# LN statistics of both possible token values taken in the first pass, and a nodes' loop in a written order with the W_res product behind it

## The chip, the cores and the metric

The kernel runs on one core of one Trainium2 chip. The metric is the device time of one execution in microseconds (us). The kernel before takes 3175.62 us, the median of three runs (3175.58 to 3176.56).

## The reference, cut to what matters

There are 6250 nodes (tokens) with 256 features each, and 100000 edges sorted by destination. Four blocks follow each other, each behind a LayerNorm without weights and each added to its input:

```python
x = x + L0_gnn(layernorm(x), edges)        # graph block
x = x + L0_ffn(layernorm(x))               # FFN of the tokens with the greatest router weight
x = x + L1_gnn(layernorm(x), edges)        # graph attention block
x = x + L1_ffn(layernorm(x))               # eight experts, weighted

# L0_ffn: weights = u @ wr + br;  the k - 1 tokens of the greatest weights are chosen
#   y = (gelu(u @ w1 + b1) @ w2 + b2) * weight;   result: u + y where chosen, u elsewhere
# L1_gnn: xn = layer_norm(x, ln1_g, ln1_b)
#   h = xn @ W;  a_src, a_dst: h with att_src, att_dst, for 8 heads
#   e = leaky_relu(a_src[src] + a_dst[dst]);  alpha = softmax of e over the edges of each dst
#   out = sum of h[src] * alpha + xn @ W_res + bias;  then a LayerNorm and an FFN with gelu
```

So a token entering L1_gnn is `X + weight * y` if it was chosen, and `X` if not. Which of the two it is can only be known once the weights of all tokens are there.

## The kernel before

The nodes lie in 50 tiles of 125 (NP = 125, NT = 50). Each tile has up to 17 slots of 128 edges (SL = 17). X, the running features, stays in SBUF for all tiles.

**First pass** (about 160 to 1226 us). `edges0(t)` gathers the source rows of a tile from DRAM, one indirect DMA per slot, issued by POOL (L342) into a ring of five buffers. VectorE builds a one-hot of the destinations (L401) and TensorE sums rows into nodes with it (L404). `weigh0(t0, c)` takes the router weight of each token of a chunk of tiles, normalises X and transposes it; `ffn0(t0, c)` makes the FFN value y of every token and stores it in the DRAM table `ytab` (L477 is y's addition). `weave` interleaves the three for successive chunks. The chunks' last two (tiles 47 to 49) have their `ffn0` beside the selection.

**Selection** (1226 to 1261). `select` finds the threshold weight by rounds of counting on VectorE and TensorE; `wm` (L583) is then the weight where the token was chosen and zero elsewhere.

**Nodes' loop** (1262 to 1385). All of `ytab` is loaded back into ten Y tiles, by SP and ACT queues in turn. `mix` makes X + wm*Y (L613), and its mean and variance (bn_stats L177, bn_aggr L178) and the inverse root by Newton steps (L166 to L172), for five tiles at a time. `front` normalises on ScalarE (L623), transposes on TensorE (L627) and applies ln1_g and ln1_b on ScalarE (L629). Two products follow for each tile, `ph` with W and the two attention columns (L651) and `pr` with W_res (L653). ScalarE evicts ph into `ht` (L654), VectorE copies the attention columns (ASAD, L655) and makes `rr` = pr + bias (L656). `ht` goes to the DRAM table `htab`, `rr` to `rtab`. Running maxima of ASAD go to `ext`. The scheduler orders the engines here, and puts into this loop also the fourteen X += cst of `add_o` (L915, on POOL) that belong to the second pass. After the loop a short chain over `ext` (L672 to L692) gives a shift for the softmax and a flag `f1I`, which is read into registers for a branch (L698).

**Second pass** (1393 us to the end). It has a written order on TensorE, VectorE and ScalarE. A tile has three groups of six slots (GS = 6; the last group ends with the nodes' own rows). `fetch(s)` gathers the rows of group s from `htab` with POOL (L342) into a ring of four buffers; `fetch_tile(t)` loads the tile's destination list (`ohT`) and `rr`. VectorE turns the list into a one-hot (L766), TensorE spreads the destination terms `adsh` over the edges (`pa`, L774), VectorE forms the logits (`ad`, L806), and the weighted rows are split in high and low parts (L859, L829) and summed on TensorE (L849). Behind it in the same weave run the block's FFN (L922, L933) and the eight experts (L1020, L1038).

Of the kernel before, what the change touches and what calls it, by code (L numbers as in the profile page):

```python
# [9 lines left out]
F32 = mybir.dt.float32  # L10
# [8 lines left out]
P = 128  # L19
N = 6250  # L20
E = 100000
D = 256
# [36 lines left out]
def gnn_ffn(ctx, tc, A, out):  # L59
# [100 lines left out]
    def rs(pool, dst, src, mul, add, op0=ALU.mult, name="rs"):  # L160

        p, n = src.shape[0], src.shape[-1]
        v = pool.tile([p, n], F32, name=name + "v")
        y = pool.tile([p, n], F32, name=name + "y")
        h = pool.tile([p, n], F32, name=name + "h")
# [19 lines left out]
    wm = stat.tile([NP, NT], F32, name="wm")  # L185
    sdT = edge.tile([P, 2, NT, SL], I32, name="sdT")
# [186 lines left out]
    with ExitStack() as p1:  # L373
# [63 lines left out]
        def weigh0(t0, c):  # L437
# [3 lines left out]
            for j in range(c):  # L441
# [11 lines left out]
                nc.vector.scalar_tensor_tensor(jk, z, 1.0, f_wr, op0=ALU.mult, op1=ALU.mult, accum_out=wts[:, t:t + 1])  # L453
                pt = psum.tile([P, KD, NP], F32, name="mi")
# [3 lines left out]
                yield  # L458

        def ffn0(t0, c):  # L460
# [11 lines left out]
            for j in range(c):  # L472
                y = pool.tile([NP, 1, D], F32, name="y")
                py = psum.tile([NP, D], F32, name="py", bufs=1)
                for f in range(NF):
                    nc.tensor.matmul(py, hT[f][:, j * NP:(j + 1) * NP], f_w2[:, f, :], start=(f == 0), stop=(f == NF - 1))  # L476
                nc.vector.tensor_tensor(y[:, 0, :], py, f_b2[0:NP, :], ALU.add)  # L477
                ndma(y, ytab, t0 + j, False)
                yield


        far = wp.tile([1, NT, HEADS], BF16, name="far")
        nc.sync.dma_start(wcat[:, :, 0:D], A["L1_gnn_W"].rearrange("(k p) m -> p k m", p=P))
        nc.sync.dma_start(wcat[:, :, HA:HA + D], A["L1_gnn_W_res"].rearrange("(k p) m -> p k m", p=P))
        atts = [bcast_load(wp, A["L1_gnn_" + n].rearrange("h j -> (h j)"), D, n) for n in ("att_src", "att_dst")]
# [3 lines left out]
        b2g = bcast_load(wp, A["L1_gnn_ffn_b2"], D, "b2g")  # L489
# [3 lines left out]
        for n, k in (("ln1_g", KD), ("ln1_b", KD), ("ffn_b1", NF), ("ln2_g", KD), ("ln2_b", KD)):  # L493
            r = wp.tile([k, P], F32, name=n + "r")
# [4 lines left out]
        bo_f = wp.tile([NEXP, D], F32, name="bo_f")  # L499
        bo_p = wp.tile([NEXP, 3, D], BF16, name="bo_p")  # L500
# [4 lines left out]
        row = {n: wp.tile([L2 + NEXP, D], F32, name="bn" + n) for n in ("g", "v", "b", "m", "be")}  # L505
# [6 lines left out]
        def prepare():  # L512
# [4 lines left out]
            yield from store_dloc(wp, psum, "mi")  # L517
            for a, att in enumerate(atts):
                for k in range(KD):
                    wa = wp.tile([P, D], F32, name="wa")  # L520
# [21 lines left out]
            rs(wp, v, v, 1.0, 1e-3, name="bq")  # L542
# [35 lines left out]
        nc.vector.tensor_scalar(wts, wts, f_br[0:NP, :], None, op0=ALU.add)  # L578


        sl = p1.enter_context(tc.tile_pool(name="sl", bufs=1))
        mask = select(tc, sl, psum, wts, ident, iota, ones, upto)
        nc.vector.tensor_tensor(wm, wts, mask, ALU.mult)  # L583
        for t0, c in CHUNKS0[-2:]:
            for _ in ffn0(t0, c):
                pass


    w2 = ctx.enter_context(tc.tile_pool(name="w2", bufs=1))
    with ExitStack() as md:  # L590
# [6 lines left out]
        for t0 in range(0, NT, XC):  # L597
            Y.append(wp.tile([NP, XC, D], F32, name=f"Y{t0}"))
            ndma(Y[-1], ytab, t0, True, eng=(nc.sync, nc.scalar)[(t0 // XC) % 2])
# [5 lines left out]
        MC = 5  # L605
        spans = [(0, 1), (1, 2), (3, 2)] + [(t, MC) for t in range(5, NT, MC)]

        def mix(t0, c):

            mv = pool.tile([NP, MC, 2], F32, name="mv")  # L610
            for j in range(c):
                t = t0 + j
                nc.vector.scalar_tensor_tensor(X[:, t, :], Y[t // XC][:, t % XC, :], wm[:, t:t + 1], X[:, t, :], op0=ALU.mult, op1=ALU.add)  # L613
                bn(pool, mv[:, j, :], X[:, t, :])
            r2 = pool.tile([NP, 2, MC], F32, name="r2", bufs=3)
            rs(pool, r2[:, 0, 0:c], mv[:, 0:c, 1], 1.0 + 1e-5, 1e-10)
            nc.vector.scalar_tensor_tensor(r2[:, 1, 0:c], mv[:, 0:c, 0], -1.0, r2[:, 0, 0:c], op0=ALU.mult, op1=ALU.mult)
            return r2

        def front(t, r2, j):  # L620

            z = pool.tile([NP, D], F32, name="z")
            nc.scalar.activation(z, X[:, t, :], AF.Identity, bias=r2[:, 1, j:j + 1], scale=r2[:, 0, j:j + 1])  # L623
            pt = psum.tile([P, KD, NP], F32, name="mi", bufs=3)
            xT = pool.tile([P, KD, NP], F32, name="xT", bufs=3)
            for k in range(KD):
                nc.tensor.transpose(pt[:, k, :], z[:, k * P:(k + 1) * P], ident[0:NP, 0:NP])  # L627
            for k in range(KD):
                nc.scalar.activation(xT[:, k, :], pt[:, k, :], AF.Identity, bias=ln1_b[:, k:k + 1], scale=ln1_g[:, k:k + 1])  # L629
            return xT  # L630

        stats = [mix(*spans[0])]
        fronts = []
        for s, (t0, c) in enumerate(spans):
            if s + 1 < len(spans):
                stats.append(mix(*spans[s + 1]))
            if s == 0:
                fronts.append(front(0, stats[0], 0))
            ht = pool.tile([NP, MC, HW], F32, name="ht")
            rr = pool.tile([NP, MC, D], F32, name="rr")  # L640
            for j in range(c):
                t = t0 + j
                if j + 1 < c:
                    fronts.append(front(t + 1, stats[s], j + 1))
                elif t + 1 < NT:
                    fronts.append(front(t + 1, stats[s + 1], 0))
                xT = fronts[t]
                ph = psum.tile([NP, HA], F32, name="ph")
                pr = psum.tile([NP, D], F32, name="pr")
                for k in range(KD):  # L650
                    nc.tensor.matmul(ph, xT[:, k, :], wcat[:, k, 0:HA], start=(k == 0), stop=(k == KD - 1))  # L651
                for k in range(KD):
                    nc.tensor.matmul(pr, xT[:, k, :], wcat[:, k, HA:HA + D], start=(k == 0), stop=(k == KD - 1))  # L653
                nc.scalar.activation(ht[:, j, :], ph[:, 0:HW], AF.Copy)  # L654
                nc.vector.tensor_copy(ASAD[:, t, :], ph[:, D:HA])  # L655
                nc.vector.tensor_tensor(rr[:, j, :], pr, g_bias[0:NP, :], ALU.add)  # L656
            ndma(ht[:, 0:c, :], htab, t0, False)
            ndma(rr[:, 0:c, :], rtab, t0, False)
            e1 = pool.tile([NP, MC, 2 * HEADS], F32, name="e1")
            nc.vector.tensor_copy(e1[:, 0:c, 0:HEADS], ASAD[:, t0:t0 + c, 0:HEADS])  # L660
            nc.vector.tensor_scalar(e1[:, 0:c, HEADS:], ASAD[:, t0:t0 + c, 0:HEADS], -1.0, None, op0=ALU.mult)
            e2 = ext if s == 0 else pool.tile([NP, 2 * HEADS], F32, name="e2")
            nc.vector.tensor_reduce(e2, e1[:, 0:c, :].rearrange("p t h -> p h t"), AX.X, ALU.max)
            if s:
                nc.vector.tensor_tensor(ext, ext, e2, ALU.max)
# [30 lines left out]

        mid.close()
# [9 lines left out]


        rem = keep.tile([NP, NT, 2 * HEADS], F32, name="rem")
# [864 lines left out]
```

## Time and profile before

| quantity | value |
|---|---|
| median of three runs | 3175.62 us |
| profiled execution | 3178.92 us |
| its span | 3177.1 us |
| mean granted TensorE clock | 0.947 |
| busy: TensorE, VectorE, ScalarE, POOL | 2804.1, 2016.2, 1198.4, 1934.0 us |

The profile is of one execution. Busy time is the time in which an engine has an instruction at work; an engine can be busy for most of the span and still bind only some of the stages. Line numbers are those of the kernel before. A wait is named by the engine and tile that waited and by the one that released it last.

### The profile page before, as it was taken

How to read it: one execution, taken by the hardware profiler on the slowest of the kernel's cores; microseconds unless marked ns; L12 is line 12 of the kernel's file. 1: busy time of each engine (PE TensorE's matmuls, PEld its weight loads, DVE VectorE, ACT ScalarE, POOL GpSimd, SP SyncE). 2: the span in 40 equal slices, each digit the busy share in tenths (PEclk: the TensorE clock that was granted, in tenths of full speed). 3: DMA queues.
4: the chain of work that ended last, by engine and by line, in shares of the span. 5: the costliest groups of instructions: out<-in, count | busy, mean ns of one | idle time of the engine just before them, and what ended most of it. 6: DMA issues, size and time to landing. Idle time of an engine off the chain costs nothing.

```text
span 3177.1 us, 40496 instructions
## 1 busy us (share of the span) xinstructions
PE 2804.1 (88%) x12746; PEld 1972.1 (62%) x12746; DVE 2016.2 (63%) x5670; ACT 1198.4 (38%) x2215; POOL 1934.0 (61%) x1772
## 2 busy tenths in 40 slices
PE   6278888888888896856889999999999999999999
PEld 5246566566666675746766666666666666666665
DVE  8543444444444346947888787777778777777731
ACT  5112222212212221634555455454544545445332
POOL 0277777777777771247777666666666666666400
PEclk8689999999999898977999999999999999999999
DMA  5533333333333335356655545445454454544412
GB/s 110 165 110 110 110 112 111 112 111 111 112 112 111 112 112 124 110 152 177 181 154 155 163 125 158 141 135 163 125 163 138 135 162 125 163 138 141 125 53 60
DMA packets 263977, 412.04 MB, mean 130 GB/s; under 512 B 55449, under 2 KB 202373, under 8 KB 263710
## 3 DMA queue, kind: packets, MB, share of 16 engines
q0 software_dynamic: 81600, 226.41, 25.7%
q1 hardware_dynamic: 169062, 170.03, 18.2%
q10 hardware_dynamic: 13080, 12.80, 1.7%
q8 instruction: 106, 1.74, 0.2%
q14 instruction: 129, 1.06, 0.1%
HBM read 376.61 MB, written 33.24 MB: 129 GB/s over the span
## 4 chain that ended last, share of the span: by engine, by line
PE 46%; DVE 6%; ACT 2%; issue 1%; DMA 1%; POOL 1%; DVEq 0%; ACTq 0%; SPq 0%; POOLq 0%
PE ph L1020 19%; PE py L1038 9%; PE iotaP L849 5%; PE py L933 5%; PE ph L922 5%; DVE hrow L839 1%; PE mi L895 1%; PE mi L960 1%; DVE lo L829 1%; POOL hrow L342 1%; PE pa L774 1%; DVE bnst L177 0%; DVE oh L861 0%; ACT hi L859 0%; DMA hrow<-htab,sdT 0%
## 5 line engine op out<-in xcount | busy, mean ns | idle before, releaser
L342 POOL DMA_INDIRECT hrow<-htab,sdT x850 | 1023.4, 1204 | 496.1 <-issue 214.2
L342 POOL DMA_INDIRECT rows<-gtab,sdT x850 | 808.1, 951 | 258.7 <-issue 125.8
L404 PE MATMUL ps<-rows,oh 128*125 128x257 f32 x1700 | 474.6, 416 | 84.8 <-DMA rows<-gtab,sdT 72.7
L1021 ACT ACTIVATE h<-ph,bi,sc 128x500 f32<-128x500 f32 (+3 forms) x448 | 321.6, 723 | 539.0 <-PE ph L1020 538.8
L404 PEld LDWEIGHTS ps<-rows,oh 128*125 128x125 f32 x1700 | 321.1, 201 | 229.6 <-DMA rows<-gtab,sdT 143.3
L1020 PE MATMUL ph<-h,W 128*128 128x500 f32 (+3 forms) x896 | 372.6, 549 | 0.0
L1038 PE MATMUL py<-Wo,h 128*125 128x256 f32 x1600 | 370.2, 381 | 0.4 <-ACT h L1021 0.4
L1020 PE MATMUL ph<-wcat,W 128*128 128x500 f32 (+3 forms) x896 | 363.5, 544 | 2.4 <-ACT h L1021 2.3
L1038 PEld LDWEIGHTS py<-Wo,h 128*125 128x125 f32 x1600 | 297.0, 188 | 72.3 <-issue 28.1
L839 DVE TENSOR_TENSOR hrow<-hrow 128x768 f32<-128x768 f32 x300 | 280.2, 975 | 76.4 <-ACT hrow L824 76.4
L1041 DVE SCALAR_TENSOR_TENSOR X<-py,gate,X 125x256 f32<-125x256 f32 x400 | 173.4, 477 | 203.4 <-PE py L1038 203.2
L829 DVE TENSOR_TENSOR lo<-hrow,hi 128x792 fp32r<-128x792 f32 (+1 forms) x300 | 285.3, 992 | 0.2 <-issue 0.2
L859 ACT ACTIVATE hi<-hrow 128x792 fp32r<-128x792 f32 (+1 forms) x300 | 236.7, 823 | 123.7 <-DVE hrow L839 123.2
L849 PE MATMUL iotaP<-hi,oh 128*125 128x264 f32 x850 | 252.0, 329 | 0.0
L1020 PEld LDWEIGHTS ph<-wcat,W 128*128 128x128 f32 x896 | 160.6, 192 | 140.2 <-issue 109.8
L1020 PEld LDWEIGHTS ph<-h,W 128*128 128x128 f32 x896 | 160.2, 195 | 106.3 <-issue 95.8
L849 PE MATMUL iotaP<-lo,oh 128*125 128x264 f32 x850 | 219.7, 291 | 4.9 <-DVE lo L829 4.8
L467 PE MATMUL ph<-xT,f_w 128*128 128x500 f32 (+3 forms) x448 | 191.4, 553 | 0.5 <-ACT xT L457 0.5
L922 PE MATMUL ph<-xT,h_w 128*128 128x500 f32 (+3 forms) x448 | 186.3, 558 | 4.3 <-ACT hT L924 3.3
L476 PE MATMUL py<-f_w,hT 128*125 128x256 f32 x800 | 182.8, 381 | 1.2 <-DVE y L477 0.4
L933 PE MATMUL py<-h_w,hT 128*125 128x256 f32 x800 | 177.6, 380 | 0.0
L849 PEld LDWEIGHTS iotaP<-lo,oh 128*125 128x125 f32 x850 | 162.5, 191 | 20.6 <-issue 7.9
(305 smaller groups left out, 3742.5 us busy)
## 6 DMA issues: line engine op xcount, KB each, us to landing
W<-in_L_ffn_W SPq DMA_DIRECT2D x224, 256.0 KB
Wo<-in_L_ffn_Wo SPq DMA_DIRECT2D x112, 256.0 KB
ohT<-dltab SPq DMA_DIRECT2D x50, 535.5 KB
rows<-gtab,sdT POOLq DMA_INDIRECT x850
hrow<-htab,sdT POOLq DMA_INDIRECT x850
hrow<-htab SPq DMA_DIRECT2D x50, 115.5 KB
X<-in_x ACTq DMA_DIRECT2D x10, 560.0 KB
ytab<-y SPq DMA_DIRECT2D x50, 112.0 KB
```

What stands on the lines that cost most here:

```text
L342: nc.gpsimd.indirect_dma_start(out=dst, out_offset=None, in_=tab, in_offset=bass.IndirectOffsetOnAxis(ap=idx, axis=0))
L404: nc.tensor.matmul(ps, oh[:, i, :], rows[:, i, :], start=(s0 + i == 0), stop=(s0 + i == SL - 1))
L467: nc.tensor.matmul(ph[:, 0:n], f_w1[:, k, f * P:(f + 1) * P], xT[:, k, 0:n], start=(k == 0), stop=(k == KD - 1))
L829: nc.vector.tensor_tensor(L["lo"][:, c], L["rows"][:, c], L["hi"][:, c].bitcast(F32), ALU.subtract)
L839: nc.vector.tensor_tensor(h4, h4, rows[:, c, D:, None].to_broadcast([P, GS // 2, HEADS, HD]), ALU.mult)
L849: nc.tensor.matmul(tiles[t]["ps"], L["oh"][:, i, :], r[:, i, :], start=(g + i + q == 0), stop=(g * GS + i == SL - 1 and q == 1))
L859: nc.scalar.activation(L["hi"][:, c], L["rows"][:, c], AF.Copy)
L922: nc.tensor.matmul(ph[:, 0:n], h_w1[:, k, f * P:(f + 1) * P], C["xT"][:, k, 0:n], start=(k == 0), stop=(k == KD - 1))
L933: nc.tensor.matmul(py[:, i, :], C["hT"][f][:, j * NP:(j + 1) * NP], h_w2[:, f, :], start=(f == 0), stop=(f == NF - 1))
L1020: nc.tensor.matmul(ph[:, 0:n], w[:, k, f * P:(f + 1) * P], rhs[:, k, 0:n], start=(k == 0), stop=(k == KD - 1))
L1021: nc.scalar.activation(h[:, f, 0:n], ph[:, 0:n], AF.Relu, bias=cols[1][:, f, e:e + 1], scale=cols[0][:, f, e:e + 1])
L1038: nc.tensor.matmul(py[:, i, :], hidden[u, "2"][:, k, j * NP:(j + 1) * NP], weights[u, "Wo"][:, k, :], start=(k == 0), stop=(k == KD - 1))
```

## The change

Three things are done.

1. In the first pass, `weigh0` keeps the mean and the variance of each normalised token in `mv2`, and `ffn0` forms x2 = X + weight*y and takes its mean and variance too. `roots_of` turns the variances into inverse roots for both cases. After the selection a blend by the mask leaves the right pair of scale and shift for each token in `r2`, so the nodes' loop takes no statistics. The router's bias is added chunk by chunk.
2. The nodes' loop has a written order on TensorE, VectorE, ScalarE and POOL. One in three normalisations and one half of each gain run on VectorE. ASAD is copied from `ht` for five tiles at a time, and the maxima are taken at tiles 20, 40, 48 and 50. The W_res product is taken out: it follows, for two tiles at a time, after the maxima's chain and before the branch, from the transposed tiles, which are kept in the Y buffers (`xTs`). The attention terms `adsh` are made inside that stage (`terms`).
3. The pool `w3` with the ring of the second pass is opened ahead of the nodes' loop. The gathers of its first four groups are issued right behind the loop, and the first tile's one-hot is made there. In the second pass two of three fetches stand half a step earlier.

The core of the diff:

```diff
@@ weigh0
+                nc.vector.tensor_copy(mv2[:, 0, t, 0:1], mv[:, 0:1])
+                nc.vector.scalar_tensor_tensor(mv2[:, 0, t, 1:2], mv[:, 1:2], r1[:, 2:3], r1[:, 2:3], op0=ALU.mult, op1=ALU.mult)
...
+            nc.vector.tensor_scalar(wts[:, t0:t0 + c], wts[:, t0:t0 + c], f_br[0:NP, :], None, op0=ALU.add)
@@ ffn0
                 ndma(y, ytab, t0 + j, False)
+                t = t0 + j
+                x2 = pool.tile([NP, D], F32, name="x2", bufs=1)
+                nc.vector.scalar_tensor_tensor(x2, y[:, 0, :], wts[:, t:t + 1], X[:, t, :], op0=ALU.mult, op1=ALU.add)
+                bn(pool, mv2[:, 1, t, :], x2)
                 yield
+        def roots_of(a, b, name):
+            rs(wp, r2[:, :, 0, a:b], mv2[:, :, a:b, 1], 1.0 + 1e-5, 1e-10, name=name)
+            nc.vector.scalar_tensor_tensor(r2[:, :, 1, a:b], mv2[:, :, a:b, 0], -1.0, r2[:, :, 0, a:b], op0=ALU.mult, op1=ALU.mult)
@@ around the selection
-        nc.vector.tensor_scalar(wts, wts, f_br[0:NP, :], None, op0=ALU.add)
+        roots_of(0, CHUNKS0[-2][0], "ra")
+        ready.close()
         sl = p1.enter_context(tc.tile_pool(name="sl", bufs=1))
         mask = select(tc, sl, psum, wts, ident, iota, ones, upto)
...
+        roots_of(CHUNKS0[-2][0], NT, "rb")
+        nc.vector.tensor_tensor(wm, wts, mask, ALU.mult)
+        nc.vector.tensor_tensor(part, r2[:, 1], mask[:, None, :].to_broadcast(both2), ALU.mult)
+        nc.vector.tensor_scalar(mask, mask, -1.0, 1.0, op0=ALU.mult, op1=ALU.add)
+        nc.vector.tensor_tensor(r2[:, 0], r2[:, 0], mask[:, None, :].to_broadcast(both2), ALU.mult)
+        nc.vector.tensor_tensor(r2[:, 0], r2[:, 0], part, ALU.add)
@@ nodes' loop
+        mid.enter_context(tc.manual_schedule(engines={PE, DVE, Activation, Pool}))
-                nc.vector.scalar_tensor_tensor(X[:, t, :], Y[t // XC][:, t % XC, :], wm[:, t:t + 1], X[:, t, :], op0=ALU.mult, op1=ALU.add)
-                bn(pool, mv[:, j, :], X[:, t, :])
-            rs(pool, r2[:, 0, 0:c], mv[:, 0:c, 1], 1.0 + 1e-5, 1e-10)
...
+        def norm(t):
+            r, m = (r2[:, 0, q, t:t + 1] for q in range(2))
+            zs[t] = pool.tile([NP, D], F32, name="z", bufs=4)
+            if t % 3 == 2:
+                nc.vector.tensor_scalar(zs[t], X[:, t, :], r, m, op0=ALU.mult, op1=ALU.add)
+            else:
+                nc.scalar.activation(zs[t], X[:, t, :], AF.Identity, bias=m, scale=r)
...
+        def gain(t):
+            pt = pts.pop(t)
+            nc.scalar.activation(xTs[t][:, 0, :], pt[:, 0, :], AF.Identity, bias=ln1_b[:, 0:1], scale=ln1_g[:, 0:1])
+            nc.vector.tensor_scalar(xTs[t][:, 1, :], pt[:, 1, :], ln1_g[:, 1:2], ln1_b[:, 1:2], op0=ALU.mult, op1=ALU.add)
...
+        steps = ((8, <X + wm*Y of the tile>),
+                 (0, product), (3, turn), (-1, evict), (2, gain), (5, norm))
+        for i in range(-8, NT + 1):
+            for lead, f in steps:
+                if 0 <= i + lead < NT:
+                    f(i + lead)
+        for k in range(len(ring)):
+            fetch_edges(k)
+        nc.vector.tensor_scalar(ext[:, HEADS:], ext[:, HEADS:], -1.0, None, op0=ALU.mult)
+        first_onehot()
@@ behind the maxima's chain, ahead of the branch
+        for t in range(0, NT, 2):
+            pr = psum.tile([NP, 2, D], F32, name="pr")
+            for i in range(2):
+                for k in range(KD):
+                    nc.tensor.matmul(pr[:, i, :], xTs[t + i][:, k, :], wcat[:, k, HA:HA + D], start=(k == 0), stop=(k == KD - 1))
...
+            nc.vector.tensor_tensor(rr[:, j:j + 2, :], pr, g_bias[0:NP, None, :].to_broadcast([NP, 2, D]), ALU.add)
+            if j == 2 or t + 2 == NT:
+                ndma(rr[:, 0:j + 2, :], rtab, t - j, False)
+            if t == 10:
+                terms()
@@ second pass
-            if s >= 1:
+            if s >= 2 and (s - 1) % NG == 0:
                 fetch(s + len(ring) - 2)
...
+            if s >= 1 and s % NG != 0:
+                fetch(s + len(ring) - 1)
```

## The prediction

> **What bounds the kernel now.** I read the page's busy shares first, then a table of stretches, because shares are averages over stages with different limits. A row of the table has the stretch, its length, the busy time of each engine in it, the granted TensorE clock, the DMA share and GB/s.
>
> ```profile
> PE 2804.1 (88%) x12746; PEld 1972.1 (62%) x12746; DVE 2016.2 (63%) x5670; ACT 1198.4 (38%) x2215; POOL 1934.0 (61%) x1772
> ```
>
> ```profile
> core 0: us, PE busy (x) PEld busy (x) DVE busy (x) ACT busy (x) POOL busy (x), PEclk, DMA share, GB/s
> 160.00:1200.00 1040.00, 896.33 (x3473) 633.63 (x3472) 446.78 (x1948) 215.57 (x432) 788.37 (x829) 0.94 0.39 111
> 1226.00:1262.00 36.00, 16.52 (x88) 14.33 (x88) 27.82 (x84) 3.02 (x9) 1.09 (x4) 0.72 0.69 166
> 1262.00:1270.00 8.00, 0.00 (x0) 0.00 (x0) 8.00 (x42) 0.00 (x0) 0.00 (x0) 0.50 1.09 247
> ...
> 1300.00:1340.00 40.00, 34.06 (x163) 26.91 (x161) 39.83 (x188) 25.79 (x65) 9.44 (x5) 1.00 0.37 109
> 1340.00:1384.00 44.00, 43.31 (x215) 36.27 (x216) 18.94 (x73) 32.41 (x83) 11.78 (x5) 1.00 0.40 119
> 1388.00:1413.00 25.00, 0.00 (x0) 0.00 (x0) 6.76 (x17) 0.00 (x0) 13.47 (x14) 0.51 0.65 170
> ...
> 1443.00:1600.00 157.00, 126.85 (x746) 110.61 (x746) 120.60 (x281) 81.50 (x152) 116.33 (x100) 0.87 0.65 182
> ...
> 1800.00:3040.00 1240.00, 1232.60 (x5555) 819.90 (x5554) 962.91 (x2088) 595.25 (x928) 782.93 (x628) 1.00 0.50 142
> ```
>
> From 1800 us TensorE is full: nothing there can be moved by this change. The nodes' loop is VectorE-bound to 1340 and TensorE-bound after. From 1388 to 1413 TensorE does nothing: the second pass waits for its first gathers and first one-hot. The first pass (160 to 1200) looks loose on every engine, but its timeline on POOL says otherwise:
>
> ```profile
> 601.67 0.95 POOL L342 DMA_INDIRECT rows<-gtab,sdT  x1 [0.30 <-issue]
> 602.93 1.10 POOL L342 DMA_INDIRECT rows<-gtab,sdT  x1 [0.30 <-PE ps L404]
> 604.34 0.95 POOL L342 DMA_INDIRECT rows<-gtab,sdT  x1 [0.30 <-PE ps L404]
> ```
>
> A gather every 1.25 us (0.95 and 0.30 to issue) without a longer pause: 829 gathers fill 1040 us. POOL's issue paces the first pass; TensorE and VectorE have slack.
>
> **First pass.** Each tile gains on VectorE a copy and a small product (0.15 and 0.16 us, like L414 and L170), x2 (0.48, like L432), and bn_stats with bn_aggr (0.42 and 0.18): 1.4 us, 70 us over the pass. VectorE is busy 43% of it, so the cover is the gathers' pace; if VectorE were the pace it would cost all 70. What can leak through is a gather that gets longer. The row: of 830 gathers, 14 took over 1.0 us, 2.2 us too much in all, and ten of these fell on the X product of L432 and its bn_stats, which come 50 times (the 1.10 above is one; L432 ran at 602.73). So 50 new pairs x 10/50 x 0.16 = 1.6 us. The rule against it: the Trainium skill (SBUF — State Buffer, "Who interferes with whom") says that a VectorE instruction with two SBUF inputs contends with a GpSimd instruction that reads SBUF, and that the later one blocks for the whole of the other. By it each x2 could hold the gathers for its 0.48: 24 us. I take the row, 1.6, and keep 24 for the range.
>
> **Tail and select.** The gathers end at 1204; then VectorE's chain counts. In the compiled order the roots of tiles 0 to 46 (12 operations of 125x94, 0.22 each, by the 125x50 rows of 0.19 to 0.24) stand ahead of the last tile's one-hot: +2.7. Inside the threshold search come x2 and bn of three tiles (3.2) and the last roots (2.5); about 2.1 of these fill the 0.7 us in which VectorE waits for TensorE's counts in each round: +3.6. After the search come four operations of 0.2 to 0.27: +1.1. With the gathers' 1.6 the search ends 9 us later: 1261.4 becomes 1270.4. Bounds 3 (all in waits) and 13 (nothing in waits).
>
> **Y loads: a new wait.** Before, SP and ACT issue them from 1240 and they land under the search. In the changed order all ten stand behind the last operation after the search, since their buffers are now those that it uses: 6.25 MB start at 1270.4. Queued behind them on SP are only the htab stores, 15 us away; ACT's engine waits too, but has nothing else then; h_w1, h_w2 and the first one-hot's load are ahead and land under the search. The first two blocks (1.25 MB at the 247 GB/s of the 1262:1270 row: 5.1 us, and 1.7 to land, like the hrow load at 1393.54) are there at 1277.2. Then X 0.48, z 0.59, transposes 0.4, the two half gains 0.45 and 0.28 (VectorE's waits for ACT's in the compiled order) and handoffs, 1 us: first product at 1280.4. Later blocks come at 0.5 us a tile, which is faster than the loop.
>
> **Loop.** These rows give its pitch:
>
> ```profile
> L629 ACT ACTIVATE xT<-mi,ln_bc,ln_gc 128x125 f32<-128x125 f32 x100 | 40.1, 452 | 25.1 <-PE mi L627 25.0
> L623 ACT ACTIVATE z<-X,r 125x256 f32<-125x256 f32 x50 | 29.6, 593 | 35.5 <-DVE r L617 35.3 <-DVE rsh L171 0.2
> L915 POOL TENSOR_TENSOR X<-X,cst 125x1024 f32<-125x1024 f32 x11 | 26.1, 2368 | 70.5 <-ACT z L623 43.9 <-DVE rsh L171 15.3 <-DVE X L613 7.2
> L613 DVE SCALAR_TENSOR_TENSOR X<-Y,wm,X 125x256 f32<-125x256 f32 x50 | 24.9, 500 | 0.4 <-DVE wm L583 0.4
> L654 ACT ACTIVATE ht<-ph 125x264 f32<-125x264 f32 x50 | 19.2, 385 | 7.8 <-PE ph L651 7.5
> ```
>
> TensorE: the tile's pitch in 1340:1384 is 2.0 us; the W_res product is 0.87 of it (32 matmuls of the same 256 columns, L933, take 6.99), so 1.13 stays. ACT: 0.39 + 0.45 + 2/3 of 0.59 = 1.23. VectorE: X 0.48, a third of a 0.40 normalisation, gain 0.28 (between L655's 0.165 for 16 columns and L656's 0.41 for 256), copies and maxima 0.08: 0.97. But POOL's 14 X+=cst still run in the loop, and they stop VectorE:
>
> ```profile
> 1327.28 2.37 POOL L915 TENSOR_TENSOR X<-X,cst 125x1024 f32<-125x1024 f32 x1 [7.95 <-DVE rsh L171]
> ```
>
> ```profile
> 1327.57 2.10 DVE L172 SCALAR_TENSOR_TENSOR rsy<-rsh,rsy 125x5 f32<-125x5 f32 x1
> ```
>
> A 0.15 us operation took 2.10, to POOL's end. Summed over the loop's small operations by their normal 0.15, such excess is 15 us of POOL's 29.9. The same rule of the skill would give all 29.9: (48.5 + 29.9)/50 = 1.57 us a tile; the row gives (48.5 + 15)/50 = 1.27. I take 1.35, nearer the row, a little up because the X products are now a larger part of what VectorE meets POOL with. 50 x 1.35 = 67.5: last eviction at 1348.5, against 1383.6.
>
> **W_res product.** It moves behind the loop. The maxima's chain comes first (1385.4 to 1388.2 before): 1351.8. Its 25 additions (some 0.7 each, twice L656's columns) and 13 pairs of rtab stores on SP run beside it; nothing waits behind these stores but the second pass's own loads. 50 x 0.87 = 43.7 us on TensorE alone, with 3.5 lost while VectorE makes terms() (7 us, of which two free PSUM buffers cover 3.5): 1399. The last addition and the branch, 4 us (before: 1388.1 to 1392.8, with its flag read at the end; now the flag is old): 1403. So product and loop together take what they took; the branch comes some 10 us later than before.
>
> **What is won** lies behind the branch. POOL's gathers of the first four groups (23 x 1.25 = 29 us) start when htab is stored, at 1351, and end at 1380 under the product; the first one-hot and terms() are done too. Before, the first VectorE step of the second pass (ad, L806) ran at 1413.8:
>
> ```profile
> PEld L774 <- DVE ohT L766: 26.6, 1, 26.6
> ...
> DVE ohT L766 <- DMA rr<-rtab: 13.6, 1, 13.6
> ```
>
> TensorE waited 26.6 us for the first one-hot, and that 13.6 for the loads issued with it. Now ad runs at 1403: -10.8. The gathers' lead (before, rows of group 2 came at 1428.5) and the earlier fetches in the ramp (1443:1600, TensorE 81%) I put at 2. On SP the second pass's loads follow the branch as before. Weights: first used at 1467, issued at 1399; 10 us later and 11 earlier leaves 45. Sum: -13, made against the profiled execution (3178.9, span 3177.1 and 1.8 around it), which stands 3.3 above the median; the difference goes onto the median: 3175.6 - 13 = 3162.6.
>
> **Rivals.**
> 1. The loop's gain is eaten by blocking: 1.57 us a tile (+11) and the late bound of the select (+4) give about 3177. For it: the 2.10 above; against it: only half of POOL's time hit VectorE before, when VectorE was at 99.6%.
> 2. The gathers are held by x2 (the slower side). Place: the first pass, POOL's pace. Price: 0.48 x 50 = 24 instead of 1.6, +22: 3185. It decides from 0.26 us a tile (13/50). For it: POOL has no slack at all there. Against it: the 602.93 row, a stretch of 0.15 only, in one pair of five.
> 3. More is won: loop at 1.2 us (-7.5) and the ramp, where POOL is busy 116 of 157 us plus 30 of issue, takes up more of the gathers' lead (-8): 3147.
> 4. The change doesn't do what it says: the gathers stay behind the branch. Not so in the compiled order; they stand ahead, and the flag's read waits for none of them.
>
> **How the numbers follow.** Forecast 0.50 (own range -5 to -21: 3155 to 3171), rival 1 0.20, rival 2 0.15, rival 3 0.15. About 0.2%, 6.4 us, is what a measurement can tell from no change. Faster: 0.45 of the forecast and rival 3, 0.60. Same: 0.05 of the forecast and 0.11 of rival 1. Slower: the rest of rival 1 and rival 2, 0.24. Range 3143 to 3186: rival 3 with some room below, rival 2 above.
>
> **What would show it.** Right: gathers of the first pass still 1.25 us apart; first X of the loop near 1277; last eviction near 1348; 23 gathers ahead of the branch; ad near 1403. Wrong: rows gathers above 1.0 us in the mean (rival 2); POOL's X+=cst with a VectorE operation of 2 us beside each (rival 1); TensorE waiting in the W_res product; an ad at 1403 but a second tile end no earlier than before, which would mean that the ramp, not the start, sets the pace.

## The result, and the profile after

The changed kernel takes 3190.98 us (median of 5 runs, 3189.86 to 3193.59), the kernel before 3175.58: a ratio of 1.0051, 95% interval 1.0036 to 1.0066. It is slower, where 3162.6 was forecast; the range ended at 3186. The profiled execution has a span of 3191.8 us, 14.7 more than before.

The busy shares of the page and the table of stretches (columns as in the prediction) stand against those of before:

```profile
PE 2805.2 (88%) x12746; PEld 1975.2 (62%) x12746; DVE 2068.1 (65%) x5677; ACT 1169.0 (37%) x2149; POOL 1926.3 (60%) x1772
```

```profile
core 0: us, PE busy (x) PEld busy (x) DVE busy (x) ACT busy (x) POOL busy (x), PEclk, DMA share, GB/s
160.00:1200.00 1040.00, 889.60 (x3442) 632.83 (x3443) 501.35 (x2170) 213.70 (x429) 787.88 (x830) 0.93 0.39 112
...
1262.00:1270.00 8.00, 1.20 (x4) 0.99 (x4) 6.87 (x26) 0.00 (x0) 1.09 (x4) 0.50 0.48 159
1270.00:1300.00 30.00, 2.70 (x10) 2.33 (x10) 10.70 (x36) 0.00 (x0) 0.00 (x0) 0.50 0.80 194
1300.00:1340.00 40.00, 37.77 (x182) 28.77 (x183) 37.09 (x77) 32.69 (x84) 18.56 (x10) 0.93 0.50 133
...
1388.00:1413.00 25.00, 21.28 (x85) 18.07 (x86) 11.07 (x16) 0.00 (x0) 11.12 (x11) 0.86 0.61 168
...
1443.00:1600.00 157.00, 121.03 (x727) 105.86 (x728) 125.49 (x288) 76.79 (x145) 111.48 (x96) 0.85 0.62 174
1800.00:3040.00 1240.00, 1232.72 (x5564) 819.61 (x5563) 962.50 (x2074) 597.58 (x934) 793.87 (x638) 1.00 0.50 143
```

VectorE did 55 us more in the first pass and POOL kept its pace there; the hole in TensorE at 1388 to 1413 is filled. But a new one has come: from 1262 to 1300 TensorE works 4 us of 38. The second pass from 1800 on is what it was. So the loss lies in places, and these moments (us from the start of the span) say in which:

| | before | predicted | after |
|---|---|---|---|
| first gather of the first pass | 134.9 | 134.9 | 144.2 |
| last gather of the first pass | 1202.9 | 1204.5 | 1210.3 |
| threshold search begins | 1226.2 | | 1243.2 |
| search and what follows it end | 1261.4 | 1270.4 | 1280.7 |
| first X product of the loop | 1262.0 | 1277.2 | 1287.8 |
| first eviction for htab | 1274.8 | (first product 1280.4) | 1304.2 |
| last eviction for htab | 1383.6 | 1348.5 | 1368.7 |
| last W_res product ends | 1384.5 | 1399 | 1424.3 |
| ad, first step of the second pass | 1413.8 | 1403 | 1430.6 |
| from ad to the end of the span | 1763.3 | 1761 | 1761.2 |

A moment is where an instruction starts, but for the rows that say "end". The last row is the point: nearly all that was gained or lost lies ahead of ad, and ad came 16.8 later instead of 10.8 earlier. Four places carry it.

**The start.** ACT's timeline, before and after (start, duration, engine or its queue, line, operation):

```profile
21.57 12.24 ACTq L82 DMA_DIRECT2D X<-in_x  x9
33.84 1.28 ACT L292 ACT_TABLE_LOAD   x1 [33.84 <-DMA X<-in_x]
```

```profile
21.34 20.11 ACTq L82 DMA_DIRECT2D X<-in_x  x9
41.49 1.28 ACT L291 ACT_TABLE_LOAD   x1 [41.49 <-DMA bnm<-in_L_ffn_m]
```

and SP's timeline after:

```profile
24.82 0.38 SPq L140 DMA_DIRECT2D att_src<-in_L_gnn_att_src  x1
...
39.38 0.29 SPq L522 DMA_DIRECT2D bnbe<-in_L_ffn_be  x1
```

The new pool "ready" gave 19 small parameter loads other buffers. Before, the loads went out at 145 to 163; now they go out at 24.8 to 39.4, among the loads of X. (That the old buffers overlapped the start's, and so had to wait, is the likely reason; no run tried it.) The last nine of ACT's fourteen X issues took 7.9 us longer, and the statistics of the start that ACT makes behind them came as much later.

The view merges the issues into one line; the trace's semaphore events say what lengthened it. A semaphore is here the counter by which a load tells that it has landed. The loads of ACT and of SP use the same eight counters, and an issue waits until the load that had its counter before has landed. In the changed kernel the X issue at 33.15 follows the landing of the small load att_dst at 33.13, and the last one, at 41.14, that of bnm at 41.12. Before, the counters that ACT waited for there were those of earlier blocks of X.

**The tail.** TensorE's timeline behind the last gather:

```profile
1214.13 2.33 PE L403 MATMUL ps<-rows,oh 128*125 128x257 f32 x10
1221.33 0.68 PE L457 MATMUL mi<-ident,z 125*128 125x125 f32 x2 [4.87 <-ACT z L449]
1222.46 0.68 PE L457 MATMUL mi<-ident,z 125*128 125x125 f32 x2 [0.45 <-ACT z L449]
1222.93 6.96 PE L403 MATMUL ps<-rows,oh 128*125 128x257 f32 x22
```

The last gather was issued at 1210.3, but 22 products of the last tile began only at 1222.9. VectorE made their one-hots at 1221.7 and 1223.0 (before: at 1204.7 and 1208.8, around the end of the gathers), behind the statistics and root chains of two tiles in its queue:

```profile
1221.70 0.92 DVE L400 TENSOR_TENSOR oh<-sdT,iotaP 128x750 f32<-128x750 f32 x1
...
1223.02 0.79 DVE L400 TENSOR_TENSOR oh<-sdT,iotaP 128x625 f32<-128x625 f32 x1
```

**The Y loads.** VectorE waits for Y as forecast. ACT waits 12 us longer: its normalisations stand behind its own ten load issues.

```profile
1280.91 18.77 ACTq L82 DMA_DIRECT2D Y<-ytab  x10
1300.09 1.09 ACT L678 ACTIVATE z<-X,r 125x256 f32<-125x256 f32 x2 [47.41 <-DMA Y<-ytab]
```

```profile
1287.82 2.46 DVE L718 SCALAR_TENSOR_TENSOR X<-Y,wm,X 125x256 f32<-125x256 f32 x6 [7.14 <-DMA Y<-ytab]
...
1301.96 0.41 DVE L689 TENSOR_SCALAR Y<-mi,ln_gc,ln_bc 128x125 f32<-128x125 f32 x1 [10.95 <-ACT Y L688]
```

ACT's wait in brackets is put down to the DMA, but the first X product was there at 1288.3. What ends at 1299.7 is the issue of the tenth load, and ACT's first work follows 0.4 us later. The line with x10 does not mean that an issue is long. Narrower windows of ACT's timeline show the same ten:

```profile
1280.91 2.45 ACTq L82 DMA_DIRECT2D Y<-ytab  x4
1288.02 0.84 ACTq L82 DMA_DIRECT2D Y<-ytab  x2
1293.90 1.15 ACTq L82 DMA_DIRECT2D Y<-ytab  x2
1298.84 0.84 ACTq L82 DMA_DIRECT2D Y<-ytab  x2
```

One issue lasts 0.3 to 0.9 us, all ten 4.3. Between them ACT waits for landings: each Y tile is loaded by two issues, ACT uses four of the eight counters here, and so each tile waits for the landing of ACT's last but one. By the semaphore events the large parts of ACT's first three Y tiles landed at 1288.00, 1293.88 and 1298.82, each 0.02 us ahead of the issue that waited for it. ACT stood for loads to land, though not for data that its next instruction needed.

**The W_res stage.** TensorE's timeline there:

```profile
1391.72 32.55 PE L779 MATMUL pr<-wcat,Y 128*125 128x256 f32 x136 [5.91 <-DVE rr L783]
1429.28 0.42 PE L832 MATMUL pa<-adsh,ohT 126*128 126x48 bf16 x6 [5.01 <-DVEq L790]
```

It stands 5.9 us while VectorE makes terms() in one piece, and 5.0 at the branch.

### The profile page after: what moved, and what is told of

Same layout as the page of the kernel before. It is cut to its first block, busy times and chain, and to the rows that moved or that the text cites. A ratio compares the mean times of both kernels' runs of the same rounds, so it can differ in the third digit from the quotient of the medians.

```text
span 3191.8 us, 40378 instructions
## 1 busy us (share of the span) xinstructions
PE 2805.2 (88%) x12746; PEld 1975.2 (62%) x12746; DVE 2068.1 (65%) x5677; ACT 1169.0 (37%) x2149; POOL 1926.3 (60%) x1772
## 4 chain that ended last, share of the span: by engine, by line
PE 46%; DVE 6%; ACT 1%; issue 1%; DMA 1%; POOL 0%; DVEq 0%; SPq 0%; ACTq 0%; POOLq 0%
PE ph L1080 19%; PE py L1098 9%; PE iotaP L909 5%; PE py L993 5%; PE ph L982 5%; DVE hrow L899 1%; PE mi L955 1%; DVE lo L887 1%; PE mi L1020 1%; PE pa L832 1%; DVE oh L921 0%; DVE bnst L174 0%; DMA hrow<-htab,sdT 0%; DVE X L995 0%; DVE w L867 0%
## 5 line engine op out<-in xcount | busy, mean ns | idle before, releaser
L403 PEld LDWEIGHTS ps<-rows,oh 128*125 128x125 f32 x1700 | 324.4, 202 | 219.5 <-DMA rows<-gtab,sdT 135.7
L400 DVE TENSOR_TENSOR oh<-sdT,iotaP 128x750 f32<-128x750 f32 x150 | 130.2, 887 | 73.9 <-PE ps L403 73.9
```

The costliest lines, as they stand in the source:

```text
L403: nc.tensor.matmul(ps, oh[:, i, :], rows[:, i, :], start=(s0 + i == 0), stop=(s0 + i == SL - 1))
```

## The experiments

Theory A: these are separate delays on one path, each with its own cause, and each comes back at ad when its cause is taken away. The rival, in each case: another limit stands right behind, and the time stays. Times above before are differences of the medians within one batch of runs; the ratio is given with its interval. All kernels start from the changed one (15.4 above before). The intervals are some 3 to 5 us to either side, and where ratio and difference disagree most (e2, e12) it is by 2 to 3 us. One stage, unchanged, also differs from profile to profile: in the six kernels that have the changed kernel's first pass the last gather stands between 1208.8 and 1211.9, and in those that have its second pass ad is 1760.4 to 1766.1 from the end. So a difference of a few us is read at the place of the edit, and not from the totals.

| | above before, us | ratio and 95% interval | ad, us |
|---|---|---|---|
| the changed kernel | +15.4 | 1.0051, 1.0036 to 1.0066 | 1430.6 |
| e1 loads held | +13.5 | 1.0040, 1.0026 to 1.0054 | 1426.6 |
| e2 Y from SP | +12.5 | 1.0047, 1.0033 to 1.0062 | 1423.7 |
| e3 terms spread | +11.5 | 1.0032, 1.0018 to 1.0047 | 1419.9 |
| e4 no statistics | +5.3 | 1.0017, 1.0008 to 1.0025 | 1417.5 |
| e5 loads after branch | +12.4 | 1.0039, 1.0025 to 1.0053 | 1426.4 |
| e6 roots late | +15.7 | 1.0048, 1.0031 to 1.0064 | 1430.9 |
| e7 Y early | -1.3 | 0.9994, 0.9985 to 1.0003 | 1409.7 |
| e8 gathers behind | +31.2 | 1.0101, 1.0084 to 1.0118 | 1427.6 |
| e9 one-hots first | +7.3 | 1.0026, 1.0016 to 1.0036 | 1419.4 |
| e10 no constant | +8.5 | 1.0024, 1.0014 to 1.0033 | 1422.6 |
| e11 four repairs | -14.0 | 0.9952, 0.9936 to 0.9969 | 1400.1 |
| e12 and Y on SP | -11.4 | 0.9954, 0.9937 to 0.9970 | 1400.5 |
| e13 and constant to o | +0.1 | 0.9998, 0.9989 to 1.0008 | 1391.3 |

**The start, e1 and e5.** One-element copies on VectorE make the small loads wait; e1's copies read the start's statistics, e5's the router's weights, which come behind the first branch. Each kernel has one of the two lines.

```diff
+        def late(t, rows=1):
+            nc.vector.tensor_copy(t[0:1, 0:1], nmr[0:1, 0:1])             # e1
+            nc.vector.tensor_copy(t[0:1, 0:1], iotaP[0:1, P:P + 1])       # e5
+            return t
...
-            r = tmp.tile([k, P], F32, name=n + "r")
+            r = late(tmp.tile([k, P], F32, name=n + "r"))
```

> The small parameter loads of the second block (attention vectors, norms, batch-norm rows) wait, by a one-element copy on VectorE, for the end of the start stage, instead of going out on SP from 24.8 us while X is still being loaded. Theory A (four separate delays, each on the path): ScalarE's last X load is issued near 33.8 instead of 41.5 us, the first gather starts near 135 instead of 144.2, and the time falls by 7 to 9 us to about 3183. Rival B (the loss is VectorE's extra work in the first pass and the selection): the gathers start earlier, but the selection does not, and less than 3 us comes back.

> As e1, but the one-element copies that hold the small parameter loads now read the router's weights, which SP loads only behind the first branch: the loads can no longer stand ahead of the last gtab stores. Theory A (separate delays on the path, each handed on one to one): ACT's table load at 33 us, first gather at 135 us instead of 144.2, last gather near 1201, everything behind it 9 us earlier, 3182. Rival (the loads now hold up the weights of the first pass or TensorE's small transposes in it, so that the gathers lose what they gained): last gather at 1206 or later, 3187 or more.

In both, ACT's table load was back at 33.1 and 34.2 us: the loads' early issue did make the X issues late. In e1 the first gather came at 138.6 only, since on SP the loads stood ahead of the last two gtab stores. In e5 it came at 135.7 (8.5 back), but the last gather at 1206.5 (3.8 back). Of the 4.7 lost between, some 3.3 went in the first fifty gathers: the five fills of the "bn" buffers now stood among the gathers, where POOL has no slack (1.3), and a few gathers beside the late loads came up to 0.7 us late. The rest is no more than the pace differs by. Both give 4 us at ad, so the loads alone give back about half of the start's delay. With POOL's fills left ahead (in e11 and e12, which have the same first pass) the last gather stood at 1205.5 and 1202.2.

**The statistics, e4, e6 and e9.**

> Leaves out all statistics of the token values: the copies to mv2, x2 and its mean and variance, both roots and the blend; scale and shift are the constants 0.5 and 0. Everything else is as in the changed kernel. It prices all that the statistics cost. Theory A: the gathers keep their pace of 1.25 us, so only the tail behind the last gather and the selection get shorter, 8 to 11 us together: about 3181. Rival B: the statistics are the whole loss, 15 us or more: 3176 or less.

```diff
-                x2 = pool.tile([NP, D], F32, name="x2", bufs=1)
-                nc.vector.scalar_tensor_tensor(x2, y[:, 0, :], wts[:, t:t + 1], X[:, t, :], op0=ALU.mult, op1=ALU.add)
-                bn(pool, mv2[:, 1, t, :], x2)
...
-        roots_of(CHUNKS0[-2][0], NT, "rb")
+        nc.vector.memset(r2[:, 0, 0], 0.5)
+        nc.vector.memset(r2[:, 0, 1], 0.0)
```

Without any statistics the last gather stood at 1209.2 (after: 1210.3): the 1 us between is less than the pace differs by without any edit, so the gathers owe the statistics nothing that can be told. But from the last gather to the search it took 24.5 us instead of 32.9 (before: 23.2). The statistics cost the tail 8.4 and the search with its blend 2; ad came 13.1 earlier.

> Only the inverse roots of tiles 0 to 46 are moved: one call for all 50 tiles behind the last feed-forward part, inside the threshold search, instead of one ahead of the last one-hot and one in the search. Theory A: the 12 small operations (2.7 us) ahead of the last tile's work were on the path, the search starts near 1238 to 1240 instead of 1243.2, ends near 1275.5; 3187. Rival (the tail is set by TensorE's changed order and the statistics themselves): the search starts where it did, or gets longer by what the tail lost; 3191.

```diff
-        roots_of(0, CHUNKS0[-2][0], "ra")
...
-        roots_of(CHUNKS0[-2][0], NT, "rb")
+        roots_of(0, NT, "rb")
```

Theory A fell here. The search began at 1243.2, as without the edit, and the one-hot moved by 0.4 us. The 12 operations had run in the gaps between the dependent small operations of the two tiles' own chains.

> Only the order of the first pass's tail is changed: the three one-hots and products of the last tile are written ahead of the normalisation of tiles 47 and 48, so that on VectorE they no longer stand behind the two tiles' statistics and root chains. Theory A (the tail grew because TensorE's 22 products of the last tile, 7.6 us, waited for one-hots that the new statistics had pushed back in VectorE's queue): the search starts near 1235 instead of 1243.2, all behind it 8 us earlier, 3183. Rival (the statistics' own time on VectorE is what lengthens the tail): 2 us at most, 3189.

```diff
+        for _ in range(len(groups)):
+            next(firsts[-1][1][0])
         for _ in zip(firsts[-1][1][0], weigh0(*CHUNKS0[-2])):
             pass
```

TensorE's timeline in e9:

```profile
1212.77 7.12 PE L403 MATMUL ps<-rows,oh 128*125 128x257 f32 x32
```

The 32 products that the changed kernel made in two groups are made in one go, 10 us before its second group. The search began at 1233.6, 23.7 behind the last gather: with all the statistics in, the tail is as short as before the change. Not their time, but where they pushed the one-hots in VectorE's queue was the price.

**The Y loads, e2 and e7.**

> All ten Y tiles are loaded from SP's queue, none from ScalarE's. Theory A: ScalarE no longer stands behind its own ten load issues (18.8 us), its first normalisation comes some 10 us earlier (near 1290 instead of 1300.1) and the time falls by 9 to 11 us to about 3181. Rival C (the loop's start is set by the bytes of Y, 6.25 MB at some 250 GB/s): the first normalisation moves by at most 2 us and the time by at most 2.

```diff
-            ndma(Y[-1][0:NP], ytab, t0, True, eng=(nc.sync, nc.scalar)[(t0 // XC) % 2])
+            ndma(Y[-1][0:NP], ytab, t0, True)
```

ACT's first normalisation came at 1286.9 instead of 1300.1, 0.7 us behind the first X product: its own issues had held it. Only 6.6 us of this were left at the last eviction, since the table stores stood behind the 20 issues on SP and ACT's evictions waited for them:

```profile
1280.87 21.31 SPq L82 DMA_DIRECT2D Y<-ytab  x20
1303.28 15.84 SPq L84 DMA_DIRECT2D htab<-ht  x6
```

> The buffers of the threshold search get a place of their own, so the ten Y loads no longer wait for its last operation (to make room, the first pass keeps three one-hot buffers instead of four and one scratch buffer instead of two). Theory A: Y is there when the search ends, the first X product follows the last operation of the blend at once (1281 instead of 1287.8), ACT's first normalisation comes near 1283 instead of 1300.1; the loop of 65 us ends 14 to 17 us earlier, ad near 1415, 3175. Rival (the loop's end is set by what POOL's X+=cst and VectorE have to do, wherever ACT starts): the loop lasts longer by as much, ad after 1425, 3186 or more.

```diff
     with ExitStack() as p1:
+        sl = p1.enter_context(tc.tile_pool(name="sl", bufs=1))
         wp = p1.enter_context(tc.tile_pool(name="w1", bufs=1))
...
         ready.close()
-        sl = p1.enter_context(tc.tile_pool(name="sl", bufs=1))
```

```profile
1257.46 21.11 ACTq L82 DMA_DIRECT2D Y<-ytab  x10
1279.97 1.09 ACT L678 ACTIVATE z<-X,r 125x256 f32<-125x256 f32 x2 [28.90 <-DVE r L607]
```

Issued from 1257 under the search, the loads hold nothing: the first normalisation stood at 1280, the last eviction at 1347.7 instead of 1368.7. The time fell by 16.7 us (+15.4 to -1.3), as forecast for it. This one place is as large as the whole loss against before. (In the profile ad came 20.9 earlier, some 2 of it because the search began earlier.)

**The W_res stage, e3.**

> The sixteen VectorE steps of the attention terms are put one behind each of the W_res additions from the sixth on, instead of all in one place. Theory A: TensorE's stall of 5.9 us in the W_res product goes, the branch comes 5 to 6 us earlier, time about 3185. Rival D (TensorE's lost time there is made up in the second pass's ramp, which is set by its own chain): under 2 us.

```diff
-            if t == 10:
-                terms()
+            if t >= 10:
+                next(parts, None)
```

TensorE no longer waited for the additions, ad came 10.7 us earlier (some 2 of them from the start and the search, which vary by that), but the time fell by only 3.9: from ad to the end this profile took 1766 us, the most of the kernels with the prefetch. e1, whose second pass is that of the changed kernel, took 1765, so this may be no more than the difference between profiles.

**The prefetch, e8.**

> Only the prefetch is undone: the edge gathers of the first four groups stand behind the branch again, as before the change, with the first one-hot still ahead. Theory A (the prefetch is worth a little, since the ramp is paced by POOL): first gather of the second pass at 1430 instead of 1372.5, first hi near 1443 instead of 1437.7, second pass longer by 5 to 10 us; 3196 to 3201. Rival (the ramp takes up the lead in any case): 3191 within 2. Rival 2 (the lead is worth all its 29 us): 3220.

```diff
-        for k in range(len(ring)):
-            fetch_edges(k)
         nc.vector.tensor_scalar(ext[:, HEADS:], ext[:, HEADS:], -1.0, None, op0=ALU.mult)
...
         for k in range(len(ring)):
+            fetch_edges(k)
             own_rows(k)
```

```profile
1427.71 0.97 POOL L341 DMA_INDIRECT hrow<-htab,sdT  x1 [65.92 <-PE pa L830]
```

```profile
1448.31 0.36 PE L830 MATMUL pa<-adsh,ohT 126*128 126x48 bf16 x5 [19.77 <-DVE ad L862]
```

Slower by 15.8 us, between Theory A and the second rival. From the first of these gathers to the end it took 1779.5 us, and before the change 1781.5 (3177.1 - 1395.6): without the prefetch the second pass counts from its first gather. From ad it is 1779.6 in e8 and 1761.2 with the prefetch. So the gathers' lead of 58 us on ad is worth 16 to 18.

**The constant, e10.**

> Leaves out the addition of the constant to X on POOL (14 instructions, which the compiled order puts into the nodes' loop; the output lacks that constant). Prices the blocking between POOL and VectorE in the loop, which the prediction put at 0.08 us a tile above the row. Theory A (ACT's 1.23 us and VectorE's share leave 1.2 a tile without it): loop 60 us instead of 64.5 from the first to the last table eviction, ad 4 to 5 us earlier, 3186; the second pass is not changed by it. Rival (the loop waits for ACT and its chain alone): loop 64, 3191.

```diff
-            nc.gpsimd.tensor_tensor(X[:, t0:t0 + n, :], X[:, t0:t0 + n, :], cst[0:NP, None, :].to_broadcast(bc), ALU.add)
```

The group of X products, in the changed kernel and in e10 (busy us, mean ns):

```profile
L718 DVE SCALAR_TENSOR_TENSOR X<-Y,wm,X 125x256 f32<-125x256 f32 x50 | 39.2, 792 | 7.1 <-DMA Y<-ytab 7.1
```

```profile
L718 DVE SCALAR_TENSOR_TENSOR X<-Y,wm,X 125x256 f32<-125x256 f32 x50 | 23.4, 477 | 7.0 <-DMA Y<-ytab 7.0
```

From the first to the last eviction it took 56.0 us instead of 64.5, less than the 60 of Theory A. POOL's 30.6 us for the constant had added 15.8 to these products, and 8.5 to the loop. One pair of the changed kernel, POOL's operation and the product beside it:

```profile
1314.18 2.36 POOL L975 TENSOR_TENSOR X<-X,cst 125x1024 f32<-125x1024 f32 x1 [2.06 <-DVE X L718]
1314.39 2.42 DVE L718 SCALAR_TENSOR_TENSOR X<-Y,wm,X 125x256 f32<-125x256 f32 x1
```

In eleven of the fourteen a product that begins inside POOL's operation ends 0.28 us behind it. It begins 0.2 to 1.2 us into it, behind VectorE operations that POOL does not hold; that is why only half of POOL's time was lost.

**All together, e11 to e13.** e11 takes e5's loads (with the fills left where they were), e7, e9 and e3.

> Four repairs together, each at one delay: parameter loads behind the first branch (with POOL's fills left where they were), Y loads under the search, one-hots of the last tile first, and the 16 steps of the second pass's terms one behind each addition of the W_res stage. Theory A (the delays are separate and each is handed on to the end one to one): 3191 - 4 - 15.5 - 4 - 7 = 3160; ad near 1388. Rival (a second limit stands behind the first: the ramp of the second pass, where POOL's gathers and the weights' loads set the pace, takes back part): 3168 or more, with ad as early.

3164.0 us, 14.0 below before: a version that beats both kernels. The four alone had given 3.0, 16.7, 8.1 and 3.9, 31.7 in all; together they gave 29.4. Within the intervals the delays add up, so they are separate.

> As e11 (four repairs), and all ten Y loads issued from SP, none from ACT. Theory A (an engine is held by its own issues: ACT could not normalise before its tenth issue was out, at 1274.9): the first normalisation comes right behind the first X product, near 1268 instead of 1275.4, and since SP has no table stores to make before 1277, none are held up as in e2: loop ends 5 to 8 us earlier, 3157. Rival (the data are late, not the engine: the first normalisations need blocks that land at 1275 in either case, or SP's issues now end so late that the table stores wait as in e2): 3164.

```profile
1267.49 1.09 ACT L690 ACTIVATE z<-X,r 125x256 f32<-125x256 f32 x2 [18.85 <-DMA Y<-ytab]
...
1292.93 0.40 ACT L723 ACTIVATE ht<-ph 125x272 f32<-125x272 f32 x1 [8.27 <-DMA htab<-ht]
```

Both were right and cancel. The first normalisation came 7.9 us earlier, so ACT's own issues had held it; then ACT stood 8.3 us for table stores behind the Y loads on SP, of which the first was issued in time (1278.5) but took 4.1 us to issue, where e11's took 0.3. The last eviction stayed (1345.3 against 1344.5).

> As e12, and the constant is added on POOL to the attention's output o instead of to X ahead of the loop (same 14 instructions, same sizes, now inside the second pass). Theory A (in the loop each of these holds VectorE; in the second pass TensorE, busy 1232 of 1240 us, is the pace and has slack for POOL): loop 8 us shorter, second pass the same, 3150. Rival (the 33 us of POOL only move: gathers or VectorE in the second pass are held by them): second pass longer by 8 us or more, 3157 or slower.

```diff
-            nc.gpsimd.tensor_tensor(X[:, t0:t0 + n, :], X[:, t0:t0 + n, :], cst[0:NP, None, :].to_broadcast(bc), ALU.add)
+            nc.gpsimd.tensor_tensor(o[:, 0:n, :], o[:, 0:n, :], cst[0:NP, None, :].to_broadcast(bc), ALU.add)
```

The last eviction came 8 us earlier and ad 9.2, and yet the time rose by 11.5: from ad to the end 1780.9 us. The rival was right; the 30.6 us of POOL cost more in the second pass than in the loop. The traces of e12 and e13 say where it fell (busy us, mean ns):

```profile
L945 DVE TENSOR_TENSOR oh<-sdT,iota 128x750 fp32r<-128x750 f32 x150 | 133.1, 887 | 0.0
```

```profile
L945 DVE TENSOR_TENSOR oh<-sdT,iota 128x750 fp32r<-128x750 f32 x150 | 153.8, 1025 | 0.0
```

The gathers kept their mean of 1199 ns. Nine of VectorE's one-hots took 3.2 us, each beside the X += o that POOL now makes later; the 20.7 us are as much as the second pass lost. That these one-hots are the whole loss is not shown.

## Why the prediction was wrong

The moments of the table give the sum: ad was forecast at 1403 and came at 1430.6. The first five terms below make up the 27.6 but for 0.1, with 0.3 less for the maxima's chain.

- **Start, not in the sum: +5.8.** The diff moved the small parameter tiles from one pool to another, and the prediction has no term for it. The first gather came 9.3 late and the last 7.4, where 1.6 was forecast. e1 and e5 show the small loads as the cause of the first, and give back about half of the second.
- **"Tail and select", forecast +7.4 behind the gathers, measured +12: 4.5 more.** The tail grew by 9.7, the search by 1.1, the blend added 1.2. The order was seen (roots ahead of the last tile's one-hot), but the price was taken from the wrong term: the 2.7 of the roots cost nothing (e6), the two tiles' statistics ahead of the one-hot 8 to 9 (e4, e9), since what waited for it was TensorE with 7 us of products. The search itself grew by less than the forecast 3.6.
- **"ACT's engine waits too, but has nothing else then": +11.4.** This is the step that failed worst. VectorE's wait for the first blocks was right (7.1 measured, 6.8 forecast). But ACT's next instruction was the first normalisation, and it came behind the tenth issue, 18.8 us after the first, not behind the first block (e2, e7, e12). From the end of the search to the first product, which started at 1302.1, it took 21.4 us instead of 10.
- **Loop, forecast 68.1 from the first product to the last eviction (1280.4 to 1348.5), measured 66.6: -1.5.** This term was right. The row gave 1.27 us a tile and 1.35 was taken; the evictions came 1.32 apart (64.5/49), and the blocking of 15 us was 15.8. The Trainium skill's rule (SBUF — State Buffer, "Who interferes with whom"), that the later one is held for the whole of the other, agrees with the single pair (up to 2.42 us instead of 0.47); summed over all of POOL's work it gave 1.57, which is rival 1, and that did not come. ACT's 1.23 us a tile, which the working also gives, is no floor: e10 ran at 1.14 (56.0/49).
- **W_res stage, forecast 47.2 to its last product and 4 to ad: +5.3 and +2.3.** TensorE stood 5.9 for terms(), where two PSUM buffers were to leave 3.5; its products took 46.6 instead of 43.7; the branch with the first products behind it 6.3.
- **What is won: right.** The hole in front of the second pass is gone. From ad to the end it took 1761.2, 2.1 less than before where 2 was forecast; profiles differ by more than that, so the 2 itself is not shown. The prefetch is what makes the early ad count: without it the kernel is 16 to 18 us slower (e8).
- **Rival 2, the gathers held by x2: refuted.** The row of the gathers after:

```profile
L341 POOL DMA_INDIRECT rows<-gtab,sdT x850 | 806.3, 949 | 259.5 <-issue 124.7 <-PE ps L403 99.3 <-PE py L478 9.1
```

Mean 949 ns (before 951), and 1066.2 us from the first to the last gather (before 1068.1). The rule of contention, read as 24 us here, gave nothing, and the 1.6 of the row not even that; e4 agrees. 15 gathers took over 1.0 us, before 16. Rival 4 was rightly put aside. That the kernel is slower came from no rival: it came from one stage that was not looked at, one engine's next instruction, and two terms that were too small. The range left no room for several of them at once.

With these causes repaired (e11) the kernel took 3164.0, 14.0 below before where 13 was forecast. That is in part chance: in e11 Y loads under the search and the terms are spread, which the forecast did not count on, and ACT still stands some 8 us for its issues (e12). The gain was there; the way to it was priced too low.

## What to carry to other kernels

When a load is moved or its wait gets later, ask for its issuing engine not only what else its queue carries but what its next compute instruction is: that one starts when the last issue is out, however early its own data are. And the last issue may itself wait for earlier loads to land, so look at the issues one by one before a merged line is read as one long issue. Where statistics are put into a stage with cover, look at the stage's last tile, where the cover ends, and ask what the new operations push back in the queue; a short one-hot ahead of 7 us of products is worth writing first. A tile that moves to another pool is a change of timing: its load may go out a stage earlier or later.

## What the runs showed of the hardware

- In this compiled program SP's and ACT's loads share eight landing counters, and an issue waits until the counter's previous load has landed. Ten Y-load issues of 0.3 to 0.9 us, 4.3 in all, so took ACT 18.8 us, and its next compute instruction came behind the last. From SP alone the twenty took 21.3 us (e2); there single issues lasted up to 2.1 us, and why was not tried.
- By the same counters, 19 small parameter loads on SP's queue, spread over 15 us, lengthened nine X issues on ACT's from 12.2 to 20.1 us (12.9 and 11.7 without them, e5 and e1).
- A POOL addition of 2.36 us stretched one VectorE product of 0.47 us to 2.42; 50 products of the same kind beside 850 gathers did not change these (949 ns, before 951).
- 30.6 us of POOL work cost 8.5 us in the loop and some 20 in the second pass (e13).
